# A graph layer and a mixture of experts on one core: the first slots' rows taken from a store of x by gathers, instead of by a product on TensorE

## The chip, the cores and the metric

The kernel runs on one core of a Trainium2 chip. A core has five engines with instruction queues of their own: PE (TensorE, matrix products; it loads weights beside its products), DVE (VectorE), ACT (ScalarE), POOL (GpSimd) and SP (SyncE, which here issues plain DMAs). Sixteen DMA engines move data between HBM and the on-chip memory SBUF; products land in PSUM. POOL issues the indirect DMAs: gathers of rows by a list of row numbers, and scatters that add to rows. The metric is device time in microseconds (us).

## The reference

Two layers over N = 2048 nodes of D = 256 numbers, each added to x:

```python
x = x + _L0_gnn_ref(_layernorm(x), edge_weight, edge_index, node_vec1)   # out[row] += w * xn[col], 67584 edges
x = x + _L0_ffn_ref(_layernorm(x), Wr, br, ln_g, ln_b, W1, b1, W2, b2)   # 8 experts, top 2 of 8 by xt @ Wr
# an expert: gelu(xe @ W1 + b1) @ W2 + b2, 256 -> 1024 -> 256; the two results weighted by their shares
```

The list of edges and the choice of experts are data: the kernel has to count and sort at run time.

## The kernel before

**The graph layer** turns the edges into dense blocks of the 2048 x 2048 matrix of weights (`make_cols`, `acs[c]`: 16 column blocks of 128) and multiplies them with the normalized x (`dense(blocks, b)`, L373: for two row blocks b, b+1 and a group of column blocks; `add` puts the sum on `acc` on DVE). PSUM has two buffers for such pairs. `GROUPS` cuts the 16 column blocks in five. After the loop over the edges come five pairs with group 3, then a branch (`tc.If(n_used < E)`, L593, a fallback that is not taken here), then the last pairs: five with group 4 (row blocks 0 to 9), three with all of `last`, column blocks 11 to 15 (row blocks 10 to 15).

**Routing** goes in two batches: `first_b`, the first NA = 10 row blocks, and `last_b`, the other six. For a batch: `square` and `roots` (ACT) and `scales` give the layer norm; `logits` and `best` find the two best experts (DVE); `count` and `sum_counts` count with products by triangles of ones on PE which place a token has in its expert's list; `places` splits the place into low and high parts, `enlist` makes one-hot matrices `in_lo`, `in_hi` of them, and `list_rows` multiplies these, so that `listed` holds the sorted lists of token numbers. `shares` and `set_shares` compute the two weights. `rec` holds a normalized row with its two experts and two shares (D + 4 = 260 numbers), and one store to `xr_d` a batch puts them into HBM.

**Slots.** The experts' work goes in slots of 256 tokens of one expert. The first three (`EARLY`; experts 0, 1, 2) are filled from the first batch alone, so that PE has work while the second batch is routed. A slot: its rows are gathered into `xs` (`get_rows`, two gathers of 128 rows), turned on PE and scaled into `xeT` (`head`, `scale_rows`), then `layer_1` (32 products, Gelu on ACT), `layer_2`, and a scatter that adds to `y_d` (`put_y`). `y_d` is first filled with `acc` (`scales`). Slot 0 of the early ones does not wait for a gather: `choose` (DVE) makes a one-hot matrix of 10 x 128 x 256 and `choose_rows` multiplies `rec` by it on PE, which gives the turned rows at once. Later slots take weights by SP, which reads the experts' numbers from `slot_i`.

Every engine's order is the order of the program's text, POOL's apart. The calls around the change, before:

```python
set_shares(first_b); places(first_b); roots(last_b); enlist(first_b)
pt = choose_rows(first_b); scale_rows(whole[0], pt)
list_rows(first_b)
hT = layer_1(whole[0])
early(first_b["all"])          # row numbers of the early slots, and their gathers
scales(last_b); logits(last_b); best(last_b, 0); best(last_b, 1); shares(last_b)
count(last_b); set_weights(whole[0]); head(whole[1])
layer_2(whole[0], hT, put_y, {1: lambda: sum_counts(last_b)})
places(last_b); enlist(last_b); slots(last_b["all"]); set_shares(last_b)
hT = layer_1(whole[1], {4: lambda: list_rows(last_b)})
```

## Time and profile before

| what | value |
|---|---|
| median of 3 runs | 500.94 us (499.71 to 501.01) |
| the profiled execution | 498.62 us, its span 496.8 us, TensorE clock 0.975 of full |
| PE busy | 454.1 us, 91% of the span |
| DVE, ACT, POOL busy | 276.3, 198.2, 158.0 us |
| DMA | 102.08 MB, mean 205 GB/s |
| `choose_rows` (L848) | 40 records, 8.8 us busy |
| `listed` products (L829) | 20 records in 1.28 us (first batch), 12 in 0.83 (second) |

Busy time of PE is not PE at its peak, since products overlap. An f32 product makes two records, a transpose, a bf16 and an f16 product one. In a timeline row the bracket at the end is the idle time ahead of the instruction on its engine and what ended it.

### The profile page before, as it was taken

Reading aid. Unit: us, or ns where it says so; the run is one execution under the profiler, and the core shown is the slowest. Engines: PE = TensorE matmul, PEld = TensorE weight load, DVE = VectorE, ACT = ScalarE, POOL = GpSimd, SP = SyncE. Lnnn points to the kernel's source line nnn. Section 1 sums busy time; section 2 is a strip of 40 time slices with the busy share of each in tenths; the row PEclk is TensorE's granted clock in tenths of the full one; section 3 lists DMA queues with packets and bytes.
Section 4 is the critical chain, followed back from the end, with each engine's and each line's share of the span. In section 5 each row is a group of like instructions: output and inputs, shape, how many; then the busy total and the mean of one; then the engine's idle time right before and its main releaser. Section 6 shows DMA issues by size and latency. Waiting matters only on the chain.

```text
span 496.8 us, 12099 instructions
## 1 busy us (share of the span) xinstructions
PE 454.1 (91%) x4996; PEld 388.6 (78%) x4996; DVE 276.3 (56%) x567; ACT 198.2 (40%) x482; POOL 158.0 (32%) x125
## 2 busy tenths in 40 slices
PE   1688898889999999899989999999999999999993
PEld 0567786677877878788878888888888888888882
DVE  5899999999999992358555222334323221210011
ACT  2368757663323310076462233332334333323330
POOL 5672632504040000000433343554343344421231
PEclk9987699999999999999999999999999999999998
DMA  3757767877665675983325997799999667631520
GB/s 100 241 178 230 231 182 232 271 206 223 204 202 173 206 243 195 314 287 119 108 32 155 333 310 205 224 352 369 348 330 298 164 198 220 176 70 23 155 83 29
DMA packets 84388, 102.08 MB, mean 205 GB/s; under 512 B 8240, under 2 KB 74656, under 8 KB 82208
## 3 DMA queue, kind: packets, MB, share of 16 engines
q1 hardware_dynamic: 76432, 87.61, 54.1%
q0 software_dynamic: 7856, 13.51, 11.8%
q8 instruction: 44, 0.72, 0.6%
q14 instruction: 24, 0.20, 0.1%
q10 hardware_dynamic: 32, 0.04, 0.0%
HBM read 75.11 MB, written 28.14 MB: 208 GB/s over the span
## 4 chain that ended last, share of the span: by engine, by line
PE 43%; DMA 9%; issue 2%; DVE 1%; ACT 1%; SPq 0%; POOL 0%; POOLq 0%; DVEq 0%
PE py L1035 18%; PE ph L1021 17%; DMA xs<-xr_d,to_i 7%; PE py L378 5%; PE px L848 2%; PE px L986 1%; DMA out<-y_d 1%; DMA y_rows<-out,to_i 1%; DMA out<-ys,to_i 0%; SPq L1176 0%; PE listed L829 0%; ACT b2w L1010 0%; POOL out L1056 0%; POOLq L1203 0%; DVE xeT L995 0%
## 5 line engine op out<-in xcount | busy, mean ns | idle before, releaser
L1021 PE MATMUL ph<-xeT,w 128*128 128x256 f32 (+1 forms) x576 | 122.2, 368 | 3.1 <-PEq L1161 1.3
L1035 PE MATMUL py<-w,hT 128*128 128x256 f32 x544 | 120.6, 379 | 0.0
L1023 ACT ACTIVATE hT<-ph,ec 128x256 f32<-128x256 f32 (+1 forms) x144 | 65.8, 461 | 132.7 <-PE ph L1021 79.5
L1021 PEld LDWEIGHTS ph<-xeT,w 128*128 128x128 f32 x576 | 103.9, 190 | 17.4 <-issue 3.0
L1035 PEld LDWEIGHTS py<-w,hT 128*128 128x128 f32 x544 | 102.0, 190 | 13.2
L1043 POOL DMA_INDIRECT y_d<-ys,to_i x30 | 48.8, 1627 | 121.8 <-DVE ys L1038 81.3
L378 PE MATMUL py<-xn_lo,ac 128*128 128x264 f32 x352 | 85.3, 395 | 0.0
L378 PEld LDWEIGHTS py<-xn_lo,ac 128*128 128x128 f32 x352 | 65.3, 191 | 12.6 <-issue 0.2
L325 DVE TENSOR_TENSOR hl<-k,iota_b 128x4096 bf16<-128x4096 bf16 x32 | 73.1, 2283 | 0.0
L364 PE MATMUL pa<-hl,hr 128*32 128x128 bf16 x3072 | 57.8, 237 | 12.3 <-DVE hr L340 9.0
L364 PEld LDWEIGHTS <-hr 128*32 128x32 bf16 x3072 | 50.6, 106 | 23.1 <-DVE hr L340 15.5
L1038 DVE SCALAR_TENSOR_TENSOR ys<-py,wt,b2w 128x256 f32<-128x256 f32 x34 | 16.4, 483 | 83.8 <-PE py L1035 76.3
L340 DVE TENSOR_TENSOR hr<-eq,w 128x3072 bf16<-128x3072 bf16 x32 | 56.2, 1758 | 2.0 <-ACT w L317 0.5
L953 POOL DMA_INDIRECT xs<-xr_d,to_i x38 | 39.5, 1038 | 44.1 <-DVE r L719 32.8
L995 DVE TENSOR_SCALAR xeT<-px,ec 128x256 f32<-128x256 f32 (+1 forms) x38 | 18.4, 525 | 63.1 <-PE px L986 56.8
L367 ACT COPY ar<-pa 128x512 f32<-128x512 f32 x64 | 34.7, 584 | 23.5 <-PE pa L364 17.0
L383 DVE TENSOR_TENSOR acc<-acc,py 128x528 f32<-128x528 f32 x37 | 25.8, 700 | 21.3 <-PE py L378 21.3
L378 PE MATMUL py<-xn_hi,ac 128*128 128x264 f32 x160 | 36.2, 387 | 1.4 <-DVEq L593 1.4
L240 POOL DMA_INDIRECT win_s<-in_src,at_i x8 | 13.4, 1679 | 74.6 <-DVE at_i L236 65.0
L378 PEld LDWEIGHTS py<-xn_hi,ac 128*128 128x128 f32 x160 | 30.2, 190 | 6.8 <-issue 1.8
L1010 ACT ACTIVATE b2w<-b,wt 128x256 f32<-128x256 f32 x36 | 16.3, 499 | 28.2 <-DVE wt L1008 24.0
L332 DVE TENSOR_TENSOR eq<-k,iota_b 128x1024 bf16<-128x1024 bf16 x32 | 21.8, 683 | 0.0
(210 smaller groups left out, 331.3 us busy)
## 6 DMA issues: line engine op xcount, KB each, us to landing
w<-in_L_ffn_W SPq DMA_DIRECT2D x40, 1024.0 KB, 10.6
ad<-ar SPq DMA_DIRECT2D x32, 512.0 KB, 4.2
ac<-ad SPq DMA_DIRECT2D x16, 1024.0 KB, 6.0
b<-in_L_ffn_b SPq DMA_DIRECT2D x20, 128.0 KB, 9.8
acc<-in_x SPq DMA_DIRECT2D x4, 512.0 KB, 6.2
out<-y_d SPq DMA_DIRECT2D x4, 512.0 KB, 6.2
xr_d<-rec SPq DMA_DIRECT2D x1, 1300.0 KB, 6.3
y_d<-acc SPq DMA_DIRECT2D x1, 1280.0 KB
```

Of the source, the lines that this page charges most:

```text
L325: nc.vector.tensor_tensor(hl.rearrange("p g (n t) -> p g n t", t=2), two(k2[:, 0], g, P), pair(P), OP.is_equal)
L332: nc.vector.tensor_tensor(eq.rearrange("p g (n t) -> p g n t", t=2), two(k2[:, 1], g, RK), pair(RK), OP.is_equal)
L340: nc.vector.tensor_tensor(hr.rearrange("p g i (n t) -> p (g i) n t", t=2), eq[:, :, None, :].to_broadcast([P, GH, 3, RK]), w[:, :, None, : ...
L364: nc.tensor.matmul(pa[j * RK:(j + 1) * RK, m, :], hr[:, g, i, :], hl[:, g, :], start=(i == 0), stop=(i == 2), tile_position=(0, j * RK))
L367: nc.scalar.copy(ar[:, m0:m0 + 4, :], pa)
L378: nc.tensor.matmul(pa[:, i, :DX], acs[c][:, b + i, :], xn(c), start=(c == blocks[0]), stop=(c == blocks[-1]))
L383: nc.vector.tensor_add(acc[:, b:b + 2, :], acc[:, b:b + 2, :], pa[:, :, :DX])
L953: nc.gpsimd.indirect_dma_start(out=(sets[s.set][0] if into is None else into)[:, t, :], out_offset=None, in_=(xr_d if rows is None else ro ...
L1021: nc.tensor.matmul(ph, w1[:, k, c * P:(c + 1) * P], xeT[:, k, :], start=(k == 0), stop=(k == KD - 1))
L1023: nc.scalar.activation(hT[:, c, :s.n * P], ph, AF.Gelu, bias=ec[:, c:c + 1], scale=1.0)
L1035: nc.tensor.matmul(py, hT[:, c, t * P:(t + 1) * P], w2[:, c, :], start=(c == 0), stop=(c == KH - 1))
L1043: st = nc.gpsimd.indirect_dma_start(out=y_d[:, :], out_offset=bass.IndirectOffsetOnAxis(ap=tos[s.to][:, t:t + 1], axis=0), in_=ys, in_offs ...
```

## The change

It does five things. (1) Slot 0's rows come, like the others', by a gather. For this the normalized x of the first batch is stored alone, as `x1_d` (10 blocks of 128 x 256, in three stores), as soon as it is scaled (eight blocks on ACT, two on POOL); the early slots gather 256 columns from there, and the experts and shares later by a second gather of 4 columns from `sh_d`. `choose` and `choose_rows` are gone. (2) The first batch is counted inside the second last pair of sums and, for experts 0 to 2 alone, listed inside the last one (`list_first`, 6 columns; the two-part one-hot of the low place is made first). The full list moves into slot 0's layer 1. (3) One pair of sums (group 4) moves ahead of the branch. (4) The second batch is counted inside slot 0's layer 1 (before: in its layer 2), and its one-hot matrices are made ahead of `head(whole[1])` on DVE. (5) `acc` goes to `y_d` in three stores as the row blocks are done; the full `xr_d` store of the first batch moves behind that of the second, ahead of SP's read of `slot_i`. `sum_counts` takes the total from `sel` by one more product for each block instead of from `seen_t`. Six products of the identity stand in front of slot 0's transposes (`turn_rows(whole[0], 6)`).

```diff
-    def dense(blocks, b):
+    def dense(blocks, b, between={}):
...
             for c in blocks:
+                if (i, c) in between:
+                    between[i, c]()
...
+        late.append(dense(GROUPS[4], 0))
         add(*late.pop(0))
     edges.close()
...
-            nc.tensor.matmul(s["all"], ones_b, s["seen_t"], start=True, stop=True)
+            nc.tensor.matmul(s["all"], ones_b, seen_b, start=True, stop=False)
+            for j in range(s["n"]):
+                nc.tensor.matmul(s["all"], ones_b, sel[:, j, :], start=False,
+                                 stop=(j == s["n"] - 1))
...
+        def enlist_first(s):
+            n = s["n"] * 2
+            full = [P, n, EARLY * TT]
+            s["in_1"] = in_1 = route.tile(full, F16, name="in_1", bufs=1)
+            nc.vector.tensor_tensor(in_1, s["spots"][:, 1, :, 0:1].to_broadcast(full),
+                                    each_1[:, None, :].to_broadcast(full), OP.is_equal)
...
+        def list_first(s, m0, m1):
+            for m in range(m0, m1):
+                nc.tensor.matmul(listed[:, 2, :EARLY * TT], s["in_lo"][:, m, :], s["in_1"][:, m, :],
+                                 start=(m == 0), stop=(m == 2 * s["n"] - 1))
...
-            for u in (1, 0, 2):
+            for u in range(EARLY):
                 nc.vector.scalar_tensor_tensor(tos[whole[u].to], tk[:, u, :], -1.0, to[:, u, :],
                                                op0=OP.add, op1=OP.max)
-                get_rows(whole[u], n=NA * P)
-            nc.scalar.copy(lists_0, listed[:, 0, :])
+                get_rows(whole[u], rows=x1_d, n=NA * P, cols=slice(0, D))
...
+        def turn_rows(s, warm=0):
...
+            for i in range(warm):
+                nc.tensor.matmul(pt[:, 0, :P], ident, ident, start=True, stop=True)
...
+        NL = NA // 2
+        take_seen(first_b)
+        for p in range(NL):
+            late.append(dense(GROUPS[4] if 2 * p + 2 < NA else last, 2 * p + 2))
+            sum_up(p)
+            if p > 2:
+                put_acc(*((0, 8) if p == 3 else (8, NA)))
+        roots(first_b)
+        scales(first_b)
+        x1_v = x1_d.rearrange("(b p) d -> p b d", p=P)
+        for j in range(8, NA):
+            nc.gpsimd.tensor_scalar(first_b["rec"][:, j, :D], acc[:, j, :D],
+                                    first_b["r"][:, 1, j:j + 1], first_b["ms"][:, j:j + 1],
+                                    op0=OP.mult, op1=OP.add)
+        for js in (range(0, 4), range(8, NA), range(4, 8)):
+            if js.start < 8:
+                scale_recs(first_b, js)
+            j = slice(js.start, js.stop)
+            nc.sync.dma_start(x1_v[:, j, :], first_b["rec"][:, j, :D])
+        logits(first_b)
+        best(first_b, 0)
+        best(first_b, 1)
+        shares(first_b)
+        select(first_b)
+        late.append(dense(last, NA + 2, {(1, last[0]): lambda: sum_counts(first_b)}))
+        sum_up(NL)
+        places(first_b)
+        enlist_first(first_b)
+        enlist_low(first_b, NA)
+        nc.scalar.activation(warm, eps_sb, AF.Sqrt)
+        late.append(dense(last, NA + 4, {(0, last[3]): lambda: list_first(first_b, 0, 2 * NA)}))
+        early(first_b["all"])
+        sum_up(NL + 1)
+        split_odds(first_b)
+        enlist_high(first_b)
+        sum_up(NL + 2)
+        set_shares(first_b)
+        nc.sync.dma_start(sh_d.rearrange("(b p) d -> p b d", p=P), first_b["rec"][:, :, D:])
+        for u in range(EARLY):
+            get_rows(whole[u], rows=sh_d, n=NA * P, cols=slice(D, RW))
...
         roots(last_b)
-        enlist(first_b)
-        pt = choose_rows(first_b)
-        scale_rows(whole[0], pt)
-        list_rows(first_b)
-        hT = layer_1(whole[0])
-        early(first_b["all"])
+        turn_rows(whole[0], 6)
+        enlist_rows(first_b)
+        count(first_b)
+        take_seen(last_b)
...
+        put_acc(NA, NB)
         scales(last_b)
         logits(last_b)
         best(last_b, 0)
         best(last_b, 1)
+        select(last_b)
+        hT = layer_1(whole[0], {4: list_batch_0, 7: lambda: sum_counts(last_b)})
+        scale_recs(last_b, range(NB - NA))
         shares(last_b)
         nc.scalar.activation(warm, eps_sb, AF.Gelu)
-        count(last_b)
+        places(last_b)
+        enlist_low(last_b)
+        enlist_high(last_b)
+        enlist_rows(last_b)
         set_weights(whole[0])
         head(whole[1])
-        layer_2(whole[0], hT, put_y, {1: lambda: sum_counts(last_b)})
-        places(last_b)
-        enlist(last_b)
         slots(last_b["all"])
+        split_odds(last_b)
         set_shares(last_b)
-        hT = layer_1(whole[1], {4: lambda: list_rows(last_b)})
+        put_recs(last_b)
+        put_recs(first_b)
+        layer_2(whole[0], hT, put_y)
+        hT = layer_1(whole[1], {3: lambda: list_rows(last_b)})
```

`sum_up(p)` adds a pair and squares its two blocks; `count`, `enlist` and `set_shares` are cut into the parts named above, each with the lines that it had. `list_batch_0` is `list_rows(first_b)` with the copy of the list to `lists_0` behind it.

## The prediction

> **What bounds the kernel now.** I read the chain of waits first, then the timelines of the engines between 200 and 265 us, then the launches of gathers. TensorE (PE) carries the whole chain from 206 us on. In the chain's rows the columns are start, length, what:

> ```profile
> 206.55 18.04 PE py L378 x80
> 224.91 4.56 PE py L378 x20
> 229.47 8.63 PE px L848 x40
> 238.10 1.12 PE listed L829 x20
> 239.21 6.96 PE ph L1021 x32
> 257.51 0.97 DVE in_hi L821
> 258.52 0.83 PE listed L829 x12
> 263.30 6.91 PE py L1035 x32
> ```

> The graph sums (L378) end at 229.5, then PE sorts the first slot's rows with a one-hot product (`choose_rows`, L848) for 8.63 us, lists the first batch (1.12), and starts the first slot's layer 1 at 239.21. Slot 1's layer 2 starts at 263.30; from there the slots follow each other with PE full, so time gained ahead of 263.30 should reach the end. An f32 matmul makes two records, so 20 records are ten matmuls: one of 264 columns costs 0.45 us (18.04 over 40).

> What the change leans on is in the timelines (start, length, row, idle before) and in summaries of single lines:

> ```profile
> 206.55 0.91 PE L378 MATMUL py<-xn_hi,ac 128*128 128x264 f32 x3 [1.39 <-DVEq L593]
> 444.92 0.79 PE L1021 MATMUL ph<-xeT,w 128*128 128x128 f32 x5 [0.95 <-PEq L1155]
> 218.18 0.28 DVE L719 RECIPROCAL r<-sd 128x20 f32<-128x20 f32 x1 [1.75 <-ACT sd L714]
> 92.06 0.95 POOL L240 DMA_INDIRECT win_s<-in_src,at_i  x1 [13.83 <-DVE at_i L236]
> 93.31 2.16 POOL L240 DMA_INDIRECT win_d<-in_dst,at_i  x1 [0.30 <-ACT acc L446]
> 240.13 1.02 POOL L953 DMA_INDIRECT xs<-xr_d,to_i  x1 [32.78 <-DVE r L719]
> DMA to landing us min/median/max: 2.7/2.8/2.9
> ```

> The first two are gaps that PE has at a branch. The last is for the six gathers of 240 to 248 us, when the DMA engines were nearly idle: rows land 2.8 us after the launch begins, and launches are 1.3 us apart (240.13, 241.46). The pair at 92 us shows that a launch stretches from 0.95 to 2.16 us while VectorE (DVE) runs its long bf16 products (92.37 to 97.29).

> **The change, step by step.**

> *The branch.* PE now has four matmuls (1.80 us) to do while DVE passes the branch. It ends them at 205.16 + 1.80 = 206.96, and then has its own branch. That costs between nothing and the 0.95 of L1155; I take 0.6. So the second pair of sums starts at 207.55, where before it was 206.55 + 1.80 = 208.35: 0.8 us gained (0.45 to 1.4).

> *Sums to choice.* The last add of the first ten blocks comes at 207.55 + 7.2 + 0.05 = 214.8 (215.73 before). From that add to the reciprocal it is 2.45 us now (215.73 to 218.18), giving 217.25. Then `logits` and `best(0)` take 2.56 (218.18 to 220.74), `best(1)` 1.37, `shares` and `select` 0.4: `sel` is there at 221.6. PE has meanwhile done ten matmuls (4.5) and five of the next ten (2.25): 221.5. It waits 0.15, then does 22 counting matmuls instead of 12 (12 cost 0.34; I take 0.6), five sums (2.25) and three (1.35): 225.85. DVE adds a pair (0.70), runs `places` (1.41: 230.67 to 232.08), two small products for `in_1` (0.25 each, as rows of 80 to 160 elements) and `in_lo` (1.49 whole, 1.55 in halves): 226.0. PE then lists the first three experts: 20 f16 matmuls of 6 columns. Bounds are 0.34 (12 counting matmuls) and 1.12 (L829, 128 columns); each must load other weights, as L829 does, so I take 1.1: 227.1.

> *The first gather.* From DVE's `tk` to the first launch it is 0.83 now (239.30 to 240.13): 227.95. The second launch at 229.25 meets `in_hi` on DVE (after one add and two small rows, 229.3 to 230.8). It costs 0 more (240 us, short DVE work) to 1.1 (2.16 against 0.95); one product of 1.49 us then a pause lies between, I take 0.8. Rows: 227.95 + 1.3 + 2.8 + 0.8 = 232.85. PE ends the sums (seven, 3.16) at 230.25 and six warming matmuls (1.3, at the transposes' 0.11 a record) at 231.6, then idles 1.25. Two transposes 0.25, first `xeT` on DVE 0.54, and a little for the second `xeT` and signals: layer 1 starts at about **234.0** instead of 239.21, 5.2 earlier.

> *After it.* Until slot 1's layer 2, PE before needed 263.30 - 239.21 = 24.1, with a 1.26 wait for `in_hi` at 257.3. Now: layer 1 6.91, list 1.12, the second batch's count 0.35 (13 small matmuls, 0.19 for 8 before), transposes 0.44, layer 2 6.91, layer 1 6.91, list 0.83, transposes 0.44: 23.9. The wait is gone, because `places`, `in_lo`, `in_hi` of the second batch (4.1, as 254.33 to 258.47) run on DVE from 240.9, done at 245; PE wants them at 252.3. Gain there 0.2.

> *Edits that I cost at nothing, and their cover.* ScalarE's first Gelu: the last squares end at 233.0, roots 0.5, table load 1.28, so 234.8; three `ph` buffers hold PE off it until 236.6. Slack 1.3. The store of x (1.3 MB, three parts): ScalarE ends its eight blocks at 217.8 + 4.0 = 221.8. Stores are behind weights and `y_d`; the DMA share was 1.07 at 369 GB/s until 221 and 0.14 after. 1.3 MB at that rate is 3.6 us, so landed near 225.5; the gather asks at 227.95. Slack 2.4. POOL's two blocks: between 0.50 (IOTA 128x256) and 3.03 us (its longest launch before 206), done by 223.9 at worst; x's other parts cover that. The store of shares (1280 pieces of 16 bytes; 1024 of 48 bytes landed in 3.4) is issued at 231.8 and landed at 235.5; POOL's six more launches run from 235.9 (six at 1.3 after 227.95) to 243.7, slot 0's rows there by 240.1, slot 1's by 242.7, and DVE asks at 245.0 and 246.7. Slack 4; what is late beyond it is slot 1's `xeT`, with 2.4 more before PE needs it at 249.9. The big `xr_d` stores move behind DVE's `slots` (252.3): 2.08 MB, 0.78 of which landed in 3.7, so 7.5, 259.8. POOL's launch for slot 3 waits for it with slot 1's adds behind; rows at about 264 to 268 (landing 2.8 to 5.6), used at 271. Slack 3. SyncE reads the slot registers after these stores (4.2 from 263.55 to 267.77): weights of slot 3 from 256.7, 11 us earlier than before, used at 278.

> **Sum.** 5.2 + 0.2 = 5.4 us off. The profiled execution took 498.62 (span 496.8, 1.8 around it): 493.2. Its time is 2.3 below the median of the runs, 500.94, which I take as the base: **495.5 us**.

> **Rivals.**

> *B. POOL and DVE hold each other up.* The two products put on POOL read SBUF while DVE is on the chain to `sel` (217.3 to 221.6), full of two-tensor products. The launches of 93.31 show that they interfere. If each POOL block (0.50 to 3.03) holds DVE for its length, 1.0 to 6.1 is lost; at 1.0 each, 2.0: 497.5. Against it: DVE's products there are 0.24 long, and launches at 240 to 246 beside such ones stayed at 1.0. [...]

> *C. The first gather lands as under load.* The median landing of all DMAs on `xr_d` in the run is 6.2 (longest 9.1), not 2.8, and nothing else is left for PE to do. Then 3.4 is lost: 498.9. For it: x's store and `y_d` have only just drained. Against: at 240 the same followed a 2.1 MB store, and rows landed in 2.8.

> *D. Gained, and given back at slot 3.* If the 2.08 MB store and the gather behind it take 6 us more than I say, PE waits at 271 for rows, and with that wait all is lost: 500.9. Against: slack of 3, and the DMA queues are empty before it.

> *E. Slower: x's store comes late.* PE idles from 231.6 until x has been written and read back. It breaks even when the store has landed at 227.95 + 5.4 = 233.4. The slowest weights between 190 and 300 us took 14.8 to land; if x's last part (issued 222.2) took that long behind weights and `y_d`, it lands at 237.0, 9.0 after the gather could start, 3.6 slower: 504.5. For it: the queues are full to 221 and x's store adds 1.3 MB to the same stretch. Against: 1.3 MB in `xr_d` landed in 6.3 with 0.77 MB alongside.

> **Chances.** Forecast 0.50, B 0.15, C 0.13, D 0.07, E 0.15. Three runs of the kernel before spread over 1.3 us (499.71 to 501.01), so 0.3%, 1.5 us, is what can be told from no change. Faster: forecast, B, C, 0.78; same: D, 0.07; slower: E, 0.15. Range: all the favourable bounds (branch 0.6, launch 0.8) give 494.1, and 0.6 for the spread of runs makes 493.5; upward through B, C and D to 501.0, which leaves E and the tails out. The forecast's own range is 494 to 497.

> **What would show it.** In the profile after: no L848 group; PE's gap at the branch under 1; the count at about 221.6 with PE hardly waiting; first gather launched near 228 and not waiting for a DMA; a PE idle of 1 to 2.5 us at the first slot's transposes; layer 1 near 234; no wait in front of the second list; slot 1's layer 2 near 257.9; then the same 14.3 a slot. If POOL's launch waits for x's store, E or part of it is true; if DVE's rows between 217 and 222 are stretched, B; if PE waits for rows at slot 3, D. A layer 1 starting after 238 makes the forecast wrong.

## The result, and the profile after

The changed kernel takes 495.42 us (median of 21 runs, 493.89 to 499.11) where the kernel before took 499.9 (21 runs beside them, 498.62 to 501.4): a ratio of 0.9915, 95% interval 0.9899 to 0.993. A later set gave 496.3 (five runs, 495.74 to 496.63) and 0.9925 (0.991 to 0.994). The profiled execution took 494.19 us, its span 492.4.

The timeline of PE after the change, in the stretch that the prediction worked through (start, length, row; in brackets the idle time ahead of the row and what ended it; the profile leaves out numbers in names, so that `x_d` is the store `x1_d`):

```profile
207.73 14.03 PE L382 MATMUL py<-xn_hi,ac 128*128 128x264 f32 x62 [0.30 <-PEq L598]
222.07 0.21 PE L783 MATMUL counts<-sel,before 128*128 128x80 bf16 x1 [0.31 <-DVE sel L770]
...
226.31 0.65 PE L856 MATMUL listed<-in,in_lo 128*128 128x6 f16 x20
...
230.02 1.50 PE L1012 MATMUL px<-ident 128*128 128x128 f32 x12
231.36 0.38 PE L1015 MATMUL px<-ident,xs 128*128 128x128 f32 x2
233.22 0.44 PE L1015 MATMUL px<-ident,xs 128*128 128x128 f32 x2 [1.48 <-DMA xs<-x_d,to_i]
234.30 3.74 PE L1053 MATMUL ph<-xeT,w 128*128 128x256 f32 x16 [0.64 <-DVE xeT L1027]
...
252.88 0.83 PE L879 MATMUL listed<-in_hi,in_lo 128*128 128x128 f16 x12
...
258.35 3.83 PE L1067 MATMUL py<-w,hT 128*128 128x256 f32 x17
```

The one-hot product is gone. PE now has two short waits at the first slot, 1.48 us for the second gather and 0.64 for `xeT`. Layer 1 starts at 234.30 (239.21 before), the second list waits for nothing, and slot 1's layer 2 starts at 258.35 (263.30 before): 4.95 us earlier. Measured from the work ahead of the branch it is 5.4, since that ran 0.4 to 0.5 us later in this execution (the last add of group 3 at 205.69 against 205.20). PE ends 4.8 us earlier (483.55 against 488.36), the span is 4.4 shorter, so that 0.4 was lost behind PE's last product.

On DVE and POOL, the timelines of the same execution:

```profile
219.06 0.48 DVE L755 SCALAR_TENSOR_TENSOR other<-other,iota_p 128x80 f32<-128x80 f32 x1
...
221.77 0.24 DVE L770 TENSOR_TENSOR sel<-hit 128x80 bf16<-128x80 f32 x1
...
227.00 0.16 DVE L888 TENSOR_TENSOR tk<-listed,flags 128x6 f32<-128x6 f32 x1 [0.49 <-PE listed L856]
...
228.33 1.05 POOL L980 DMA_INDIRECT xs<-x_d,to_i  x1 [8.88 <-DVE acc L387]
229.69 1.39 POOL L980 DMA_INDIRECT xs<-x_d,to_i  x1 [0.31 <-issue]
...
263.84 1.08 POOL L980 DMA_INDIRECT xs<-xr_d,to_i  x1 [6.31 <-DMA xr_d<-rec]
```

The first gather is launched at 228.33, and the wait ahead of it is not put down to a DMA: the store of x was there. The row of 0.48 us is the only one on the way to `sel` that is longer than its like (0.24). Slot 3's gather waits for the big store until 263.84, but PE finds its rows at 272.17 without a wait.

### The profile page after: what moved, and what is told of

It reads as the page before. It is cut to its first block, busy times and chain, and to the rows that moved or that the text cites. A ratio compares the mean times of both kernels' runs of the same rounds, so it can differ in the third digit from the quotient of the medians.

```text
span 492.4 us, 12148 instructions
## 1 busy us (share of the span) xinstructions
PE 447.5 (91%) x5008; PEld 382.5 (78%) x5008; DVE 273.2 (55%) x563; ACT 197.5 (40%) x480; POOL 164.0 (33%) x133
## 5 line engine op out<-in xcount | busy, mean ns | idle before, releaser
L980 POOL DMA_INDIRECT xs<-xr_d,to_i x32 | 33.4, 1043 | 15.8 <-DMA xr_d<-rec 6.3
```

Of the source, the lines that this page charges most:

```text
L980: nc.gpsimd.indirect_dma_start(out=(sets[s.set][0] if into is None else into)[:, t, cols], out_offset=None, in_=(xr_d if rows is None else ...
```

## The experiments

Twelve runs: eleven other kernels, and the changed one once more. They ran on three chips: the first four on one (the kernel before there: 500.85 us), the next four on a second (501.1), the last four, the changed kernel among them, on a third (500.1). Which chip the first set of the changed kernel had is not on record, and it was not run beside the first eight, so their medians cannot be compared closely with its 0.9915. They are also less certain: the kernel before spread over 6 us and more on the first two chips (498.75 to 504.8, 498.45 to 506.12), and over 1.8 on the third. What follows therefore rests on the traces first.

The table gives, from each kernel's profiled execution, the time from the start of the second pair of late sums (those around the branch) to layer 1 of the first slot, the time of layer 1's first 16 records, and how long the granted clock stood at 0.50 there. In the kernel with the branch move undone the second pair has no row of its own; its start is the first pair's, 209.73, and 1.80 us.

| kernel | median us | ratio to before, 95% | sums to layer 1 | first 16 records | clock at 0.50 |
|---|---|---|---|---|---|
| changed kernel, first set | 495.42 | 0.9915 (0.9899 to 0.993) | 26.57 | 3.74 | none |
| changed kernel, again | 496.3 | 0.9925 (0.991 to 0.994) | 26.74 | 3.74 | none |
| branch move undone | 499.62 | 0.9982 (0.9953 to 1.0011) | 26.88 | 6.75 | 6.8 us |
| one more gather | 499.17 | 0.9972 (0.9944 to 1.0) | 31.51 | 5.34 | 6.8 us |
| gather not from the store | 499.53 | 0.9974 (0.9947 to 1.0002) | 26.34 | 5.41 | 3.4 us |
| sorting behind the sums | 508.11 | 1.0136 (1.0092 to 1.018) | 37.34 | 5.45 | 17.1 us |
| ten blocks on ScalarE | 497.55 | 0.9968 (0.9934 to 1.0001) | 26.12 | 3.74 | none |
| no warming products | 498.88 | 0.9963 (0.9944 to 0.9981) | 27.11 | 6.34 | 6.8 us |
| list in the gap | 499.91 | 0.9983 (0.9954 to 1.0012) | 26.76 | see there | none |
| first records stored early | 497.41 | 0.993 (0.9907 to 0.9953) | 26.52 | 5.41 | 3.4 us |
| gap filled | 497.08 | 0.9948 (0.9934 to 0.9963) | 26.29 | 3.74 | none |
| filled, ScalarE, early store | 497.67 | 0.9956 (0.9939 to 0.9972) | 26.13 | 3.74 | none |
| no gathers of shares | 496.68 | 0.9928 (0.9906 to 0.9951) | 26.38 | 5.41 | 3.4 us |

### The branch move undone

```diff
-        late.append(dense(GROUPS[4], 0))
         add(*late.pop(0))
     edges.close()
...
+        late.append(dense(GROUPS[4], 0))
         for p in range(NL):
```

> The changed kernel with one part undone: the first pair of sums with group 4 stands behind the branch again. My theory: the branch gap on PE goes from 0.30 us (trace after) back to about 1.39 (trace before), everything behind it on the chain (choice, count, gather, layer 1) moves by the same, so 495.4 + 1.0 = 496.4 us (ratio to the kernel before 0.993; the changed kernel had 0.9915). Rival: the first slot hangs on something that does not move with the sums (the store of x landing, the end of ScalarE's work), then no change, 495.4.

The gap came back as 1.38 us; in the twelve traces that have the pair ahead of the branch it is 0.30 to 0.56. That is 0.8 to 1.1 us, as expected. The time went up by more, and the reason stands in the windows of PE busy time and clock (each row: stretch, its length, busy time with counts of PE, PEld, DVE, ACT and POOL, granted clock, DMA share, GB/s):

```profile
234.32:237.74 3.42, 1.60 (x13) 1.16 (x12) 0.47 (x2) 2.86 (x7) 2.54 (x3) 1.00 0.84 116
237.74:241.15 3.41, 2.77 (x8) 2.20 (x8) 3.21 (x8) 0.47 (x1) 3.00 (x2) 0.50 0.98 254
241.15:244.56 3.41, 3.41 (x10) 2.69 (x9) 2.96 (x16) 0.95 (x2) 2.57 (x3) 0.50 0.25 71
```

Behind the waits for the gather, which left PE 1.60 us of work in the stretch ahead, the granted clock stands at 0.50 for two stretches of 3.41 us, and the first 16 records of layer 1 take 6.75 us instead of 3.74. So the profiled execution (501.38) holds the gap and a fall of the clock, and the median of its 12 runs, 499.62, was not taken beside the changed kernel's. The mechanism of the move is shown; its price in the median is not.

### One more gather ahead of slot 0's

```diff
+                if u == 0:
+                    nc.gpsimd.indirect_dma_start(
+                        out=more_x,
...
                 get_rows(whole[u], rows=x1_d, n=NA * P, cols=slice(0, D))
```

> The changed kernel with one more gather (128 rows of 256 numbers into a tile that nobody reads) launched ahead of slot 0's two. My theory: PE stands idle until slot 0's second gather has landed, so one launch more ahead of it, 1.05 to 1.4 us in the trace after, comes back whole in the end: 495.4 + 1.3 = 496.7 us (ratio 0.994). Rival: PE's first slot waits for other things too (xeT on DVE, the warming products, ScalarE), so part or nothing is seen: 495.4 to 496.

The profiled execution lost 4.9 us up to layer 1, not 1.3. Its timelines of PE, POOL and SP:

```profile
233.91 0.44 PE L1025 MATMUL px<-ident,xs 128*128 128x128 f32 x2 [1.51 <-DMA xs<-x_d,to_i]
238.84 0.69 PE L1025 MATMUL px<-ident,xs 128*128 128x128 f32 x2 [4.49 <-DMA xs<-x_d,to_i]
...
232.27 1.00 POOL L990 DMA_INDIRECT xs<-x_d,to_i  x1 [0.30 <-issue]
...
231.92 0.36 SPq L1166 DMA_DIRECT2D sh_d<-rec  x1
232.33 0.62 SPq L732 DMA_DIRECT2D y_d<-acc  x1
```

Slot 0's second gather is launched at 232.27, beside SP's stores of the shares (1280 pieces of 16 bytes) and of the last 0.79 MB of `y_d`, and its rows come 6.6 us later (238.84). In the changed kernel it is launched at 229.69, ahead of these stores (231.04, 231.45), and its rows come after 3.5. This is the landing under load of rival C. The changed kernel's own trace has it as well, one gather further on: slot 0's two land 2.8 and 3.5 us after their launches, the next one, launched at 231.39 beside the same stores, 6.6 us after. The change escapes it narrowly: the second launch starts 1.4 us ahead of the first of the stores, and ends (231.08) as it is issued.

### The gather taken from x instead of from the store

```diff
-                get_rows(whole[u], rows=x1_d, n=NA * P, cols=slice(0, D))
+                get_rows(whole[u], rows=x, n=NA * P, cols=slice(0, D))
```

> The changed kernel, with the early slots' rows gathered from the input x instead of from the store of normalized rows: the values are other ones (rows without layer 1's sums and without the layer norm), the number and size of all transfers is the same, and no gather waits for the store. My theory: the store has landed before the gather is asked for, so 495.4 us, no change (0.9915). Rival E of the prediction, in part (the first gather waits for the store, or its writes still slow the reads down): 1 to 3 us faster, 492.5 to 494.5, with the first rows landing earlier than the 2.8 us after launch.

```profile
235.36 0.44 PE L1015 MATMUL px<-ident,xs 128*128 128x128 f32 x2 [1.33 <-DMA xs<-in_x,to_i]
236.44 5.41 PE L1053 MATMUL ph<-xeT,w 128*128 128x256 f32 x16 [0.64 <-DVE xeT L1027]
```

In these two rows of its PE timeline the wait for the rows is 1.33 us, from the sums' second pair to layer 1 it is 26.34: within 0.4 us of the changed kernel's 26.57 and 26.74. Launch to rows is 3.4 us (232.00 to 235.36) against 3.5. So the store costs the gather nothing, and rival E is out. The time rose because the clock fell here too (5.41 for 3.74), and because of a second effect that is described under the list in the gap.

### The sorting behind the sums

```diff
-        late.append(dense(last, NA + 2, {(1, last[0]): lambda: sum_counts(first_b)}))
+        late.append(dense(last, NA + 2))
...
-        late.append(dense(last, NA + 4, {(0, last[3]): lambda: list_first(first_b, 0, 2 * NA)}))
-        early(first_b["all"])
+        late.append(dense(last, NA + 4))
+        sum_counts(first_b)
         sum_up(NL + 1)
-        split_odds(first_b)
-        enlist_high(first_b)
         sum_up(NL + 2)
+        places(first_b)
...
+        list_first(first_b, 0, 2 * NA)
+        early(first_b["all"])
```

> The changed kernel with the counting, the places and the first list put behind all sums, so that the rows come by gather as in the changed kernel, but nothing of the sorting lies beside the sums. Same work on every engine. My theory: choose_rows' 8.63 us of PE work were not bought by the gather, but by sorting beside the sums: the chain count, places, in_1, in_lo, list, tk, launch, landing then starts at the end of the sums, about 229.6, and layer 1 starts near 241.4 instead of 234.3: 495.4 + 7 = 502.4 us, slower than the kernel before (ratio 1.005). Rival: the work taken off PE is the gain itself, and the place of the count matters little: 495 to 497.

Slower than before, 1.0136 (1.0092 to 1.018), with the same work on every engine and `choose_rows` gone as well. PE's timeline:

```profile
235.50 0.43 PE L856 MATMUL listed<-in,in_lo 128*128 128x6 f16 x10 [2.99 <-DVE in_lo L840]
...
245.47 0.69 PE L1015 MATMUL px<-ident,xs 128*128 128x128 f32 x2 [6.05 <-DMA xs<-x_d,to_i]
247.31 0.69 PE L1015 MATMUL px<-ident,xs 128*128 128x128 f32 x2 [1.15 <-DMA xs<-x_d,to_i]
248.64 5.45 PE L1053 MATMUL ph<-xeT,w 128*128 128x256 f32 x16 [0.64 <-DVE xeT L1027]
```

PE waits for the list, then for the rows. It is 10.6 to 10.8 us from the changed kernel, not 7: the gathers (launched 238.02 and 240.51) meet the two stores and land 7.4 and 6.8 us after their launch, which adds some 3.5. (The first of them starts 1.4 us ahead of the stores, 239.39 and 239.80, but its launch takes 2.18 us.) Behind the waits layer 1's first records run at a granted clock of 0.50 and take 5.45 us for 3.74, another 1.7. So the 8.63 us taken off PE are not the gain. The gain is bought by what lies beside the sums.

### Ten blocks on ScalarE

```diff
-        for j in range(8, NA):
-            nc.gpsimd.tensor_scalar(first_b["rec"][:, j, :D], acc[:, j, :D],
...
-        for js in (range(0, 4), range(8, NA), range(4, 8)):
-            if js.start < 8:
-                scale_recs(first_b, js)
+        for js in (range(0, 4), range(4, 8), range(8, NA)):
+            scale_recs(first_b, js)
```

> The changed kernel with all ten blocks of the first batch scaled on ScalarE, none on POOL. My theory: POOL and DVE hold each other up little (one DVE row of 0.48 instead of 0.24 us in the trace after), and the store of x, whose last part then leaves about 1 us later, still lands before the gather asks: 495.4 - 0.2 = 495.2 us (0.991). Rival B of the prediction: POOL's two blocks cost the chain 1 us or more: 494.4 or less. Rival: the later store is seen: 496 or more.

The row of 0.48 us is 0.24 here, `sel` starts 13.74 us after the second pair's start instead of 14.04, and PE no longer waits for it. Rival B thus has a size: 0.3 us, of which one row of 0.24 is seen stretched. The later store was not seen at the gather. The 0.3 cannot be looked for in the times. The profiled execution, 495.9, is the fastest of the twelve, although PE waits in it 0.77 and 0.34 us for slot 3's rows (launched at 266.44, not 263.84). Seven of the twelve took 495.9 to 497.73 and five 500.99 to 501.87, and no trace of the slower five was kept.

### No warming products

```diff
-        turn_rows(whole[0], 6)
+        turn_rows(whole[0])
```

> The changed kernel without the six products of the identity ahead of slot 0's transposes. My theory: they lie in an idle stretch of PE (1.5 us of it are left after them) and do nothing for the time: 495.4 us (0.9915). Rival: PE's idle time of then 3.2 us in one piece lowers the granted clock or makes the next products slower: 0.3 to 1 us slower, with longer rows for the transposes and layer 1 behind the gap.

The rival was right in kind, and too small. Windows of 3.41 us, laid so that the fall begins with one (columns as above):

```profile
229.85:233.26 3.41, 0.61 (x3) 0.20 (x2) 0.99 (x3) 2.35 (x7) 2.80 (x3) 1.00 0.67 119
233.26:236.67 3.41, 2.60 (x7) 1.84 (x8) 2.52 (x4) 0.51 (x1) 2.80 (x3) 0.50 1.09 212
```

PE was busy for 0.61 us in the stretch 229.85 to 233.26, the clock stood at 0.50 for the next 6.8 us, and layer 1's first 16 records took 6.34, 2.6 us more than at full clock. The six products do no needed work, but they are 1.50 us of PE work (230.02 in the trace after) in the place where this kernel has the 0.61 ahead of the fall. They are not always enough: with them the clock fell in four of seven traces (see below).

### The first batch's list in the gap

```diff
+        enlist_rows(first_b)
-        turn_rows(whole[0], 6)
-        enlist_rows(first_b)
+        turn_rows(whole[0], 6, lambda t: list_rows(first_b, t * NA, (t + 1) * NA))
...
         def list_batch_0():
-            list_rows(first_b)
             nc.scalar.copy(lists_0, listed[:, 0, :])
```

> The changed kernel with the first batch's full list (20 products, 1.28 us on PE in slot 0's layer 1) moved into PE's idle time at slot 0's transposes, ten products behind each pair of transposes, and DVE's product for it (1.48 us) moved ahead of slot 0's xeT, where DVE was idle for 2.69 us. My theory: the wait for the second gather (1.48 us) and the wait for xeT (0.64) take the 1.28 us, so 495.4 - 1.1 = 494.3 us (0.989). Rival: the list's first half waits for DVE until after the rows have landed and pushes the second transposes and xeT: no gain or 0.3 slower.

Timeline of PE, and a row of DVE's:

```profile
232.31 0.72 PE L879 MATMUL listed<-in_hi,in_lo 128*128 128x128 f16 x10 [0.73 <-DVE in_hi L872]
...
234.39 6.33 PE L1055 MATMUL ph<-xeT,w 128*128 128x256 f32 x28
...
246.91 4.15 PE L1069 MATMUL py<-w,hT 128*128 128x256 f32 x18 [1.40 <-ACT hT L1057]
...
275.34 0.41 PE L1015 MATMUL px<-ident,xs 128*128 128x128 f32 x2 [1.63 <-DMA xs<-xr_d,to_i]
...
246.33 0.26 DVE L819 TENSOR_TENSOR at_e<-hit,counts 128x96 f32<-128x96 f32 x1 [7.21 <-PE py L1069]
```

The list does fit into the gap, and layer 1 ends 1.1 us sooner after its start. All of it is given back. `at_e`, the first row of the second batch's `places` on DVE, needs PE's counting products, which ended at 241.05, and starts at 246.33. DVE, and ScalarE beside it, run as if PE's signals reached them up to 5.3 us late. PE then waits 1.40 for ScalarE's last `hT`, and 1.63 and 0.35 for slot 3's rows, whose store follows from `at_e`.

The same lateness between the last counting product and `at_e` is in six of the eight traces of the first two chips: 0.8 us (branch move undone), 2.3 (gather from x), 3.8 (ten blocks on ScalarE), 1.2 (no warming), 5.3 (this one) and 2.2 (records early). It ends each time 2.1 to 2.5 us after the last launch of the gathers of shares. In the two others (one more gather, sorting behind the sums) the counting ended 3.8 and 3.9 us after that launch, later than those 2.1 to 2.5, and `at_e` starts 0.04 us behind it. The lateness is not in the first trace of the changed kernel (0.04 us, 242.13 to 242.17), nor in any of the four on the third chip (0.03 to 0.04), three of which launch these gathers while they count. Whether it belongs to the chip or to the run is not shown.

### The first batch's records stored early

```diff
         put_acc(NA, NB)
+        put_recs(first_b)
...
         put_recs(last_b)
-        put_recs(first_b)
```

> The changed kernel with the first batch's xr_d store (1.3 MB) back right behind the last y_d store, about 22 us earlier, and only the second batch's (0.8 MB) ahead of SyncE's read of the slot registers. My theory: slot 3's rows and weights have slack in either place, and the store of x and y_d is over, so no change: 495.4 us (0.9915), with slot 3's first gather launched earlier than the 263.84 of the trace after. Rival D of the prediction, in some runs: PE waits for slot 3 when the 2.1 MB come late, which would be why the changed kernel's 21 runs spread over 5.2 us and the kernel before's over 2.8: then faster in the median by 0.5 to 1 us, and a smaller spread. Rival: the store now runs beside the first gathers and slows them: slower.

Slot 3's first gather left at 264.21, not earlier than the 263.84 of the trace after. But slot 0's layer 2 starts 4.7 us later here (248.12 against 243.38), so in the chain it is 4.4 us earlier. It no longer waits for the store; slot 0's adds stand in front of it on POOL until 263.11. PE did not wait for slot 3, with `at_e` 2.2 us late; it did not with `at_e` 2.3 us late in the gather from x either, so that the run does not show what the edit saved. SP's read of the slot registers halves, as the summary of `slot_i` shows, first for this kernel:

```profile
L1196 SPq TENSOR_LOAD <-slot_i x1: 3782/3782/3782, 259.4 to 259.4; - x1
```

and for the changed kernel:

```profile
L1196 SPq TENSOR_LOAD <-slot_i x1: 7539/7539/7539, 254.4 to 254.4; - x1
```

The stores ahead of it on SP are 0.8 MB here and 2.1 MB there. With the later store it is 7.5 us in the traces of ten blocks on ScalarE, the list in the gap and the changed kernel again as well (7.53, 7.56 and 7.55), and in the kernel before, with 0.8 MB, it is 3.6. The ratio, 0.993, is not told apart from the changed kernel's; the clock fell here for 3.4 us as well, so that the two runs differ in more than the edit.

### The changed kernel again

> The changed kernel itself, unaltered, on the same chip as the variants, since they all came out 2 to 4 us above what I expected and their traces show two things that the trace after does not: the granted clock at 0.50 for 3.4 or 6.8 us behind the wait for the first gather, and PE's signals to DVE and ScalarE arriving 2 to 5 us late between 239 and 248 us. Theory: both belong to the changed kernel and depend on the run, so here 496.7 us (500.9 by 0.9915) with a spread of 4 us or more, and a trace with one or both of them in some of the runs. Rival: they belong to the variants, and this run has neither: 495.5, all runs within 2 us, clock 1.00 from 232 to 250.

It came to run on the third chip, not on one of the variants'. 496.3 us; spread 0.9 us over five runs, not 4 or more; neither effect in its trace. So it does not decide between the two: chip and run differ too. Its emptiest window on the 3.41 us grid (see the last section), and the one behind it:

```profile
232.72:236.14 3.42, 1.68 (x14) 1.24 (x12) 0.56 (x2) 2.81 (x7) 2.63 (x3) 1.00 0.83 122
236.14:239.55 3.41, 2.77 (x14) 2.33 (x14) 3.21 (x8) 1.00 (x3) 2.91 (x2) 1.00 1.01 219
```

### The gap filled

```diff
+                if t == 0:
+                    for i in range(fill):
+                        nc.tensor.matmul(pt[:, 1, P:], ident, ident, start=True, stop=True)
+            if fill:
+                idle = ps_h.tile([P, TS], F32, name="ph")
+                for i in range(2):
+                    nc.tensor.matmul(idle[:, :P], ident, ident, start=True, stop=True)
...
-        turn_rows(whole[0], 6)
+        turn_rows(whole[0], 6, 5)
```

> The changed kernel with five more products of the identity between the transposes of slot 0's first and second 128 rows (1.25 us, in a wait of 1.48), and two in the wait for xeT (0.5 in 0.64). No needed work is moved. Theory: the clock falls to half when PE was busy for less than about half of one of the 3.41 us windows that the trace's clock steps keep to (1.60 us busy and less before a fall in the variants, 1.67 and more before none). In the changed kernel PE's busy time in such a window is 1.29 us at the worst phase, so some 4 of 10 runs fall, and lose 1.7 to 3.0 us in layer 1. Filled, the worst window has some 2.5: no fall, so the median 0.7 to 1.5 us below the unaltered kernel of this call, smaller spread. Rival: the clock is not the cause of the spread, or identity products do not count as work: same as the unaltered kernel, or slower by the products that come late.

```profile
232.86 1.28 PE L1019 MATMUL px<-ident 128*128 128x128 f32 x10
234.31 0.44 PE L1015 MATMUL px<-ident,xs 128*128 128x128 f32 x2 [0.17 <-DMA xs<-x_d,to_i]
...
459.50 5.99 PE L1060 MATMUL ph<-xeT,w 128*128 128x256 f32 x27 [1.39 <-issue]
```

The gap is filled, no needed product is late, and no window between 212 and 262 us has less than 3.0 us of PE work. But the time is not better: 497.08, ratio 0.9948 (0.9934 to 0.9963). PE stands still for 1.39 us ahead of 459.50, for nothing that the profile shows; the next kernel has the like (1.66 ahead of 459.32), and none of the other twelve traces, the kernel before among them, has it. It comes five records behind a branch. The filling moves all later PE instructions by 14 records; whether that has to do with it is not shown. The cause is open.

### Filled, with ten blocks on ScalarE and the early store

The edits of "The gap filled", "Ten blocks on ScalarE" and "The first batch's records stored early" together.

> The filled kernel with two more edits that were tried alone: all ten blocks scaled on ScalarE (the count came 0.3 us earlier behind the second pair of sums than in the trace after), and the first batch's xr_d store right behind the last y_d store (no wait for slot 3's rows, where two variants waited 1.1 and 2.0). Theory: the three add up: 1 to 2 us below the unaltered kernel of this call, ratio to the kernel before 0.988 to 0.990. Rival: the store beside the first gathers delays them, or ScalarE's later end delays x's last part: no better than the filled kernel.

No. Sums to layer 1 is 26.13, the clock holds there, and PE does not wait for slot 3: each part does what it did alone. The stop ahead of 459.3 (1.66 us), and the 7.49 us of the 27 records behind it, which took 5.99 in the filled kernel, take back more than that.

### No gathers of shares

```diff
-        for u in range(EARLY):
-            get_rows(whole[u], rows=sh_d, n=NA * P, cols=slice(D, RW))
```

> The changed kernel without the six gathers of experts and shares (4 numbers a row) for slots 0 to 2, so their results get the weight that the rows' initial contents give and the output lacks them. Theory: PE's signals are late only while these gathers of 16-byte pieces are under way (in the variants the lateness begins 2 to 3 us after the first launch and ends 2.2 us after the last), so without them DVE's at_e of the second batch starts within 0.1 us of the last counting product, no ScalarE wait in layer 1, and up to 1.2 us less than the unaltered kernel of this call. Rival: the lateness has another cause: at_e still 2 to 5 us late, the time the same.

`at_e` starts 0.04 us after the last counting product, but so it does in the unaltered kernel on this chip, so the run tells nothing about the late signals. It tells about the clock, in its windows:

```profile
233.05:236.47 3.42, 1.41 (x10) 0.90 (x9) 0.94 (x3) 2.78 (x7) 2.52 (x3) 1.00 0.99 110
236.47:239.88 3.41, 3.41 (x10) 2.67 (x9) 3.15 (x12) 0.70 (x2) 2.02 (x2) 0.50 1.03 282
```

Up to here PE does the same work as in the changed kernel. The windows merely fall otherwise over its two waits: 1.41 us of work in one of them, where the changed kernel's emptiest had 1.68 on the same chip, and the next runs at a granted clock of 0.50. The table's 5.41 against 3.74, 1.67 us, is the price.

## Why the prediction was right, step by step

**The branch.** Gap 0.30, where 0.6 was taken: 1.1 us gained instead of 0.8. The undone kernel confirms it (1.38).

**Sums to choice.** `sel` ended at 222.0, 14.3 us after the second pair's start; predicted 14.05. 0.24 of the difference is rival B's one stretched row (0.48 us), which takes 0.24 when POOL's two products are gone. Three rows of DVE start while POOL's products run (218.51, 218.79 and 219.06, POOL from 218.32 to 219.45), and only the last is stretched, so that a POOL product beside it is not enough to stretch a row; what more it takes is not shown.

**List, launch, rows.** The list took 0.65, not 1.1: 20 products of 6 columns do cost less than 20 of 128, which take 1.28 in the same trace. `tk` to the first launch took 1.33, not 0.83. The same small rows stand between the two in both kernels, so they are not the reason; with the sorting behind the sums it is 1.33 as well (236.69 to 238.02). POOL's wait for DVE is an instruction of its own in the trace after (it ends at 227.60, 0.73 ahead of the launch), and in the trace before none stands there; that would be the added half microsecond, but it was not tried. The second launch was stretched by 0.39, not 0.8, and its rows came 3.53 us after it began (2.8 and 0.8 were taken). The errors nearly cancel: 233.2 for the rows (predicted 232.85) and 234.30 for layer 1 (234.0).

**After it.** 234.30 to 258.35 is 24.05, predicted 23.9.

**The sum.** 5.4 us off was predicted; the profiled spans differ by 4.4, or 4.9 after allowing for the later start. The rest is 0.4 at the end of the run. The medians differ by 4.5, so the saving was forecast 0.9 too large. That 495.5 came so close to 495.42 is luck: its base of three runs, 500.94, lay 1.0 above the median of 21, and the two errors cancel.

**What was costed at nothing.** ScalarE's first Gelu came without delay, and the x store was there (gather from x). Slot 3's slack was overstated: its gather was launched at 263.84, not 259.8, because the store left SP at 253.39, not 252.3, and took some 10 us, not 7.5. Where `at_e` came 3.8 and 5.3 us late, PE did wait there, and at 2.3 it did not, so rival D is real as soon as the second batch slips by some 3 us, an estimate from these three.

**The rivals.** E is refuted. C's late landing exists (6.6 us for 3.5), but the second launch is 1.4 us ahead of the first of the stores beside which it shows. The prediction had placed that store (shares at 231.8; it came at 231.04), but not asked what it does to slot 0's gather, and it looked for the load elsewhere, in x's store and `y_d` just drained: that C did not cost anything was in part luck. That the change is only worth something with the sorting beside the sums is shown by its undoing.

**What was missing** is the clock. The step "then idles 1.25" priced PE's wait at its length. In four of the seven traces that have the changed kernel's pattern of waits (branch undone, gather from x, records early, no shares), the clock fell behind it, and cost 1.7 or 3.0 us more; in three (both of the changed kernel, ten blocks on ScalarE) it did not. How often it falls in the changed kernel's own runs stays open: the first set's spread of 5.2 us would fit, the second set's 0.9 does not ask for it. Where the kernel before waits (2.16 us of work in its emptiest window near 257 us) the clock held.

No version tried here was measurably faster than the changed kernel; but only the last three ran beside it on one chip.

## What to carry to other kernels

Work that only sorts and counts cost the chain little here while it lay beside long matrix sums (0.65 us of PE for the list), and the saving from taking a product off TensorE is real only if what replaces it has been started that much earlier: undo the order and the same instructions are slower than before. When a transfer comes onto the critical path, look at what other queues issue 1 or 2 us later, since the same gather landed in 3.5 or 6.6 us here. And price an idle stretch of TensorE by the clock behind it too: here, between 200 and 262 us, each 3.41 us window with 1.60 us of its work or less was followed by one at a granted clock of 0.50, and the 16 records of layer 1 behind it took 5.34 to 6.75 us instead of 3.74.

## What the runs showed of the hardware

**Late signals.** In six of the eight traces from two chips, DVE ran as if PE's signals reached it 0.8 to 5.3 us late, until 2.1 to 2.5 us after the last launch of the gathers of 16-byte pieces; where it was 5.3 (the list in the gap), ScalarE's last `hT` of layer 1 began at 246.38, beside `at_e` at 246.33. In the four traces from a third chip `at_e` follows the counting in 0.03 to 0.04 us. The cause is open.

**A register read by SP** took 3.6 us (before) and 3.8 (records early) behind 0.8 MB of stores, and 7.5 (four traces) behind 2.1 MB.
